# A gated MLP's adapters: two batches to a product in the ways out, both groups side by side in down's way in

## The chip, the cores and the metric

The kernel runs on one core of one Trainium2 chip. The metric is the device time of a run in microseconds (us); lower is better. Times given are the median of a few runs, and beside them stands one execution that the hardware profiler recorded.

## The reference, cut to what matters

The program is two transformer layers on 64 sequences (batches) of 32 tokens with 256 features, everything in float32. The part that is changed is the conditioning of the first layer's feed-forward: a gated MLP whose three projections each have a low-rank adapter of rank 16. Every batch has its own adapter, one of eight, chosen by an index that is known only at run time:

```python
def lora_linear(x, W, A, B, adapter_indices):
    base = einsum('bsd,df->bsf', x, W)
    lora = einsum('bsr,brf->bsf', einsum('bsd,bdr->bsr', x, A[adapter_indices]), B[adapter_indices])
    return base + lora

gate = lora_linear(x, Wg, Ag, Bg, i)      # 256 -> 1024
up   = lora_linear(x, Wu, Au, Bu, i)      # 256 -> 1024
y    = lora_linear(silu(gate) * up, Wd, Ad, Bd, i)   # 1024 -> 256
x    = x + ffn(y)
```

The text calls A the "way in" (features to 16 ranks) and B the "way out" (16 ranks to features). After this MLP come a quantised feed-forward (ffn), in the second layer a linear map with adapters, attention, a batch of experts and another quantised feed-forward.

## The kernel before, in words

The 2048 tokens are worked on in eight chunks of 256 tokens, that is of eight batches, and a chunk is two groups of four batches (128 tokens each). In a first half of some 790 us the kernel does the first layer's attention, in 32 steps. The second half is a pipeline written out by hand in `turn2(n)`: in turn n, chunk n goes through the gated MLP and the feed-forward, chunk n-1 through the second layer's attention, and chunk n-2 through its experts and last feed-forward, and the adapters of chunk n+1 are fetched. The order of the calls in `turn2` is the order of each engine's queue. A last function, `drain`, ends the chunks that are left. Chunk 0's gate and up products are done earlier, between the last steps of the first half (`chunk_0`).

Weights of the MLP (cgt, cut, cdt) stay in SBUF. The adapters don't: they are gathered anew for every chunk. `tabulate`, one piece at a time during the first half, writes two tables in DRAM with SP's DMAs: `alora`, whose row holds the ways in of gate, up and down for one feature and one adapter, and `blora`, whose rows hold the ways out of gate and up. `gather` (lines 431 and 433) copies a column of row numbers on VectorE (`at`) and then has GpSimd issue an indirect DMA. `fetch_in` gets the way in of one batch into the tile ag, `fetch_out` the ways out of one batch (128 rows of 1 KB) into the tile bx, and `fetch_down` down's way out for one group into bdt. In a turn these are eight, eight and two gathers. The row numbers (aidx, bidx, didx) are made once by `small_tables`, on VectorE, early in the first half.

The products concerned, all on TensorE:

- `adapters_in` (L472) brings the tokens to the ranks of gate and up; `adapters_spread` (L488) multiplies with a matrix fold of zeros and ones, which repeats the result in every block of 32 partitions, and masks it into u, so that gate's ranks stand in one half of the columns and up's in the other.
- `gate_up` (L507) does the full products of gate and up for one block of 128 features, and leaves the sum in a PSUM bank. Four blocks fill four banks.
- `gate_up_adapters` (L521) adds the ways out into those four banks: for each of eight batches and each of four blocks, one product with 32 rows (16 ranks of gate and of up), 128 columns of weights and 64 streamed columns (32 tokens for gate, 32 for up). The four blocks lie on four quarters of the partitions. Then ScalarE's Silu (L528) and VectorE's product (L529) make hT.
- `down_adapters` (L537) is down's way in: for two groups, eight blocks of features and four batches, one product with 16 columns of weights and 32 streamed ones, onto four quarters of the output partitions. VectorE copies the result (L546) to the diagonal blocks of ud, whose other blocks were set to zero once.
- `down` (L553) is the full product, and at its end (L559) the way out: four products with 128 columns of weights and 128 streamed ones.

Other lines that the text names: L1398 is `quant_up`, the gate and up product of the last feed-forward for chunk n-2, whose weights are y3T, a transposed tile that ScalarE copies out of PSUM (L395, `turn_y`). L1285 is the exponential of attention (`attn_exp`), L1233 a masked copy of the keys (kb), both on ScalarE. L1206 (`queries_keys`), L611 and L636 (the second layer's linear map) and L1242 (`project_values`, with its weights wv2, in the trace wv) are products that are not changed. L1047 is the last product of the first half's attention, and L1052 adds it to the tokens.

Of the kernel before, what the change touches and what calls it, by code (L numbers as in the profile page):

```python
# [15 lines left out]
P = 128  # L16
B = 64
# [8 lines left out]
for _name, _n in (  # L26
    ("ident", 128), ("pair", 64), ("cos", 32), ("sin", 32), ("cos4", 4),
    ("sin4", 4), ("causal", 32), ("blk4", 4), ("blk8", 8), ("quad", 4), ("p_mod32", 1), ("p", 1), ("p_mod16", 1),
    ("row16", 1), ("head2", 2), ("out_row", 1),
):  # L30
    _CONST[_name] = (_NCONST, _NCONST + _n)
    _NCONST += _n
# [6 lines left out]
def _constants():  # L39
# [30 lines left out]
    put("out_row", p // 32 * 256 + p // 16 % 2 * 128 + p % 16)  # L70
# [6 lines left out]
def mk_kernel(  # L77
# [61 lines left out]
    bidx = keep.tile([P, B], I32, tag="bidx", name="bidx")  # L139
    didx = keep.tile([P, NG], I32, tag="didx", name="didx")  # L140
    didf = keep.tile([P, NG], F32, tag="didf", name="didf")
# [5 lines left out]
    def small_tables():  # L147
# [7 lines left out]
        nc.vector.tensor_scalar(bidx, idx("lora"), 16.0, const("out_row"), MULT, ADD)  # L155

        folded = idx("expert")[:, :32]
        nc.vector.tensor_reduce(folded, ident.rearrange("p (r c) -> p c r", r=4), AX.X, ADD)
        nc.vector.tensor_copy(
            fold.rearrange("p (r c) -> p r c", r=4), folded.unsqueeze(1).to_broadcast([P, 4, 32])  # L160
        )
        own = idx("lora").rearrange("p (g b) -> p g b", b=4)
        of_group = keep.tile([P, NG, 4], F32, tag="m6", name="of_group")
        nc.vector.tensor_tensor(of_group, own, const("blk4").unsqueeze(1).to_broadcast([P, NG, 4]), MULT)
        nc.vector.tensor_reduce(didf, of_group, AX.X, ADD)
# [146 lines left out]
    blora = dram.tile([8 * P, 2 * P], F32, tag="blora", name="blora")  # L312
# [8 lines left out]
    def tabulate():  # L321
# [45 lines left out]
        for r in range(4):  # L367
            for i, src in enumerate((bg, bu)):
                rows = slice((2 * r + i) * P, (2 * r + i + 1) * P)
                nc.sync.dma_start(  # L370
                    out=blora[rows, :].rearrange("p (k f) -> p k f", k=2),
                    in_=src.rearrange("p (k r f) -> p k r f", k=2, r=4)[:, :, r, :],
                )
                yield
# [70 lines left out]
    def way_out(b):  # L445

        return mlp["bx", b // 4][:, b % 4 * 256 : (b % 4 + 1) * 256]

    def fetch_out(ch, b, held=True):
        gather(way_out(b), blora, bidx[:, ch * 8 + b : ch * 8 + b + 1], held)  # L450

    def fetch_down(ch, gi, held=True):

        g = ch * 2 + gi
        gather(bdt[:, gi, :], bd, didx[:, g : g + 1], held)
# [56 lines left out]
    def gate_up_adapters(ch, g):  # L512
# [4 lines left out]
        for b in range(8):  # L517
            cols = slice(b * T, (b + 1) * T)
            for r in range(4):
                rows = slice(32 * r, 32 * r + 32)  # L520
                nc.tensor.matmul(  # L521
                    banks[r].rearrange("p (i t) -> p i t", i=2)[:, :, cols],
                    lhsT=way_out(b)[rows, g * P : (g + 1) * P], rhs=c["u"][rows, :, cols],
                    start=False, stop=(b == 7),
                )
# [4 lines left out]

    def down_adapters(ch):
        c = chunks[ch]
        ps = bank()
        for gi in range(2):
            for k in range(8):
                for r in range(4):
                    nc.tensor.matmul(  # L537
                        ps[32 * r : 32 * r + 16, gi * T : (gi + 1) * T],
                        lhsT=way_in(gi * 4 + r)[:, 64 + k * 16 : 80 + k * 16],
                        rhs=c["hT"][:, k, gi * P + r * T : gi * P + (r + 1) * T],  # L540
                        start=(k == 0), stop=(k == 7),
                    )

        for r in range(4):
            rows = slice(32 * r, 32 * r + 16)
            nc.vector.tensor_copy(ud[rows, :, r, :], ps[rows, :64].rearrange("p (g t) -> p g t", g=2))  # L546

    def down(ch):
# [8 lines left out]
        for i in range(2):  # L557
            for gi in range(2):
                nc.tensor.matmul(  # L559
                    ps[:, i * 256 + gi * P : i * 256 + (gi + 1) * P], lhsT=bdt[:, gi, i * P : (i + 1) * P],  # L560
                    rhs=ud[:, gi, :, :].rearrange("p b t -> p (b t)"), start=False, stop=(i == 1 and gi == 1),
                )
# [85 lines left out]
    with ExitStack() as s1:  # L648
# [477 lines left out]
        for n in range(-1, len(steps) + 2):  # L1126
# [6 lines left out]
            if 28 <= n < 30:  # L1133
                fetch_out(0, 2 * (n - 28), False)
                fetch_out(0, 2 * (n - 28) + 1, False)
            if n == 30:
                for b in range(4, 8):
                    fetch_out(0, b, False)
# [17 lines left out]
    bdt = w.tile([P, 2, D], F32, tag="bdt", name="bdt")  # L1156
    for gi in range(2):
        fetch_down(0, gi, False)
    fetch_linear(0)
    ud = w.tile([P, 2, 4, T], F32, tag="ud", name="ud")  # L1160
    nc.gpsimd.memset(ud.rearrange("p g b t -> p (g b t)"), 0.0)
# [289 lines left out]
    def turn2(n):  # L1451
# [19 lines left out]
        for k in range(8):  # L1471
# [7 lines left out]
            elif k == 5:  # L1479
                on(n - 1, attn_exp)  # L1480
            elif k == 6:
# [55 lines left out]
        on(n + 1, fetch_out, 4)  # L1537
        on(n, ffn_down)
        on(n + 1, fetch_out, 5)
        on(n + 1, fetch_out, 6)  # L1540
        on(n + 1, fetch_out, 7)
# [7 lines left out]
        on(n + 1, fetch_down, 0)  # L1549
        on(n + 1, fetch_down, 1)  # L1550
# [126 lines left out]
```

## Time and profile before

| what | value |
|---|---|
| median of 3 runs | 1453.79 us (1450.05 to 1453.99) |
| the profiled execution's own time | 1451.43 us |
| its span, from the first to the last instruction | 1449.7 us |
| TensorE busy | 1399.7 us, 97% of the span |
| VectorE, ScalarE, GpSimd busy | 829.9, 614.1, 577.2 us |
| mean granted TensorE clock | 0.992 |
| gathers of ways in, ways out and down's way out, by the held row numbers | 954 ns of GpSimd each |

A row of the groups names the line, the engine, the operation, what is written and read, the shape (for a product rows times columns of weights and the streamed tile) and the number of instructions; behind the bar stand the busy time in us, the mean length of one in ns, and the idle time of the engine ahead of it with what ended it. PE is TensorE's multiplying, PEld its loading of weights, which overlaps it. Lengths of products overlap too, so that the time from one start to the next says more than a length.

### The profile page before, as it was taken

What the parts mean: (1) busy time and instruction counts of PE and PEld (TensorE: products, weight loads), DVE (VectorE), ACT (ScalarE), POOL (GpSimd) and SP (SyncE); (2) the same over time, 40 slices, a digit from 0 to 9 for tenths busy, and PEclk for the clock granted to TensorE, in tenths of its full rate; (3) what the DMA queues carried; (4) which work ended last, traced back from release to release, by engine and by line L of the source; (5) the groups of instructions that cost most, each with busy time, mean ns of one, the idle gap of its engine ahead of it and who ended that gap; (6) DMA issues with size and microseconds to landing.
All of it is one profiled execution on the core that took longest, in us unless ns stands there. A gap on an engine that the chain in (4) does not pass through costs nothing.

```text
span 1449.7 us, 39390 instructions
## 1 busy us (share of the span) xinstructions
PE 1399.7 (97%) x16552; PEld 1086.2 (75%) x16552; DVE 829.9 (57%) x1879; ACT 614.1 (42%) x2014; POOL 577.2 (40%) x650
## 2 busy tenths in 40 slices
PE   5899999999999999999999999999999999999996
PEld 3666777776767677767777788888887878788874
DVE  1566686867677776766565323363636262635554
ACT  1355665656575756565655512130312121212121
POOL 3423367777533333333445141524251606060320
PEclk9999999999999999999999999999999999999999
DMA  6201001321221000100001161313131304040220
GB/s 172 61 2 67 5 16 20 77 47 33 35 66 36 23 6 15 38 12 1 13 14 44 38 115 52 98 49 92 39 102 34 107 17 123 6 116 23 67 74 15
DMA packets 101625, 71.41 MB, mean 49 GB/s; under 512 B 71429, under 2 KB 88965, under 8 KB 101449
## 3 DMA queue, kind: packets, MB, share of 16 engines
q0 software_dynamic: 15744, 38.03, 9.5%
q1 hardware_dynamic: 82504, 26.34, 7.6%
q10 hardware_dynamic: 3200, 4.52, 1.0%
q8 instruction: 131, 2.15, 0.6%
q14 instruction: 46, 0.37, 0.1%
HBM read 64.54 MB, written 6.29 MB: 49 GB/s over the span
## 4 chain that ended last, share of the span: by engine, by line
PE 91%; DMA 3%; SPq 2%; DVE 2%; issue 1%; ACT 1%; POOL 0%; ACTq 0%; DVEq 0%
PE ps L779 16%; PE ps L810 15%; PE ps L1047 8%; PE ps L507 8%; PE ps L1398 5%; PE ps L578 4%; PE ps L553 3%; PE ps L1438 3%; PE ps L597 3%; PE ps L992 2%; PE ps L521 2%; PE ps L889 2%; PE ps L1206 2%; PE ps L1032 2%; SPq L276 1%; PE ps L967 1%
## 5 line engine op out<-in xcount | busy, mean ns | idle before, releaser
L433 POOL DMA_INDIRECT we<-in_ew,at x64 | 61.1, 955 | 277.5 <-DVE h L1405 203.7
L1001 ACT ACTIVATE sq<-ps 128x128 f32<-128x128 f32 x256 | 71.1, 278 | 211.6 <-PE ps L992 204.4
L793 POOL TENSOR_TENSOR qT<-ra,rb 128x256 f32<-128x256 f32 x64 | 46.6, 728 | 272.6 <-DVE rb L791 272.5
L1047 PE MATMUL ps<-wo,ogT 128*128 128x256 f32 x512 | 120.6, 389 | 6.1 <-DVE aT L896 6.1
L779 PE MATMUL ps<-hsT,wq 128*128 128x256 f32 x512 | 126.4, 390 | 0.0
L779 PE MATMUL ps<-hsT,wk 128*128 128x256 f32 x512 | 122.2, 382 | 0.0
L790 DVE TENSOR_TENSOR ra<-ps,ct 128x512 f32<-128x512 f32 x128 | 87.4, 683 | 49.9 <-PE ps L779 44.9
L810 PE MATMUL ps<-wv,hsT 128*128 128x512 f32 x256 | 115.2, 593 | 0.0
L810 PE MATMUL ps<-wg,hsT 128*128 128x512 f32 x256 | 115.1, 592 | 0.0
L1047 PEld LDWEIGHTS ps<-wo,ogT 128*128 128x128 f32 x512 | 95.8, 192 | 20.9 <-DVE aT L896 6.6
L779 PEld LDWEIGHTS ps<-hsT,wq 128*128 128x128 f32 x512 | 95.5, 192 | 18.3 <-issue 5.8
L873 DVE RECIPROCAL enz<-ps 128x256 f32<-128x256 f32 x64 | 107.5, 1721 | 2.7 <-PE ps L864 2.7
L779 PEld LDWEIGHTS ps<-hsT,wk 128*128 128x128 f32 x512 | 98.3, 192 | 13.7
L1010 POOL TENSOR_TENSOR f<-f,mhalf 128x8 f32<-128x8 f32 x32 | 53.1, 1660 | 133.5 <-DVE f L1008 133.5
L810 PEld LDWEIGHTS ps<-wg,hsT 128*128 128x128 f32 x256 | 48.6, 190 | 61.2 <-issue 54.3
L791 DVE TENSOR_TENSOR rb<-ps,ct 128x512 f32<-128x512 f32 x128 | 87.0, 680 | 0.0
L927 ACT ACTIVATE qv<-ok,nmx 128x64 f32<-128x64 f32 x256 | 85.0, 336 | 1.3 <-DVE nmx L923 1.3
L810 PEld LDWEIGHTS ps<-wv,hsT 128*128 128x128 f32 x256 | 48.6, 190 | 47.6 <-issue 45.9
L1398 PE MATMUL ps<-guT,y3T 128*128 128x352 f32 x256 | 79.5, 464 | 0.5 <-ACT y3T L395 0.5
L529 DVE TENSOR_TENSOR hT<-ps,sg 128x256 f32<-128x256 f32 x64 | 24.2, 419 | 96.9 <-ACT sg L528 96.9
L896 DVE SCALAR_TENSOR_TENSOR aT<-ps,ct 128x256 f32<-128x256 f32 x64 | 24.1, 419 | 85.6 <-PE ps L889 85.6
L433 POOL DMA_INDIRECT ag<-alora,at x56 | 53.4, 954 | 49.3 <-DVE at L431 39.3
(233 smaller groups left out, 3056.4 us busy)
## 6 DMA issues: line engine op xcount, KB each, us to landing
x<-in_x SPq DMA_DIRECT2D x8, 256.0 KB
wq<-in_wqT SPq DMA_DIRECT2D x16, 128.0 KB
wk<-in_wkT SPq DMA_DIRECT2D x16, 128.0 KB
wv<-in_wvT SPq DMA_DIRECT2D x4, 512.0 KB
wg<-in_wgT SPq DMA_DIRECT2D x4, 512.0 KB
wo<-in_woT SPq DMA_DIRECT2D x4, 512.0 KB
row<-in_wgu ACTq DMA_DIRECT2D x11, 128.0 KB
out<-res SPq DMA_DIRECT2D x5, 256.0 KB
```

Source lines behind the costliest of these rows:

```text
L433: nc.gpsimd.indirect_dma_start(out=to, out_offset=None, in_=table, in_offset=bass.IndirectOffsetOnAxis(ap=at, axis=0))
L507: nc.tensor.matmul(ps[:, i * 256 : (i + 1) * 256], lhsT=mlp[name, k // 4][:, j, part], rhs=c["xT"][:, j, :], start=(i == 0 and j == 0), st ...
L578: nc.tensor.matmul(ps[:, i * 256 : (i + 1) * 256], lhsT=wt[:, j, k * P : (k + 1) * P], rhs=yT[:, j, :], start=(j == 0), stop=(j == 1),)
L779: nc.tensor.matmul(ps[:, half * 256 : (half + 1) * 256], lhsT=wt[:, c, half * 256 + pr * P : half * 256 + (pr + 1) * P], rhs=hs[:, c, lo : ...
L790: nc.vector.tensor_tensor(by_t(a.rearrange("p h t -> p (h t)")), by_t(ps), cosb, MULT)
L791: nc.vector.tensor_tensor(by_t(b.rearrange("p h t -> p (h t)")), by_t(ps), sinb, MULT)
L810: nc.tensor.matmul(ps, lhsT=hs[:, c, lo + gi * P : lo + (gi + 1) * P], rhs=wt[:, c, :], start=(c == 0), stop=(c == 1),)
L873: nc.vector.reciprocal(t[:, e, :], banks[e][:, :256])
L927: nc.scalar.activation(qv[:, k, :], ok[:, k, :], AF.Exp, bias=nmx[:, k : k + 1], accum_out=rs[:, k : k + 1],)
L1001: nc.scalar.activation(sq, po[e][:, k * P : (k + 1) * P], AF.Square, accum_out=f[:, e * 4 + k : e * 4 + k + 1],)
L1047: nc.tensor.matmul(ps[:, gi * D : (gi + 1) * D], lhsT=s["ogT", gi][:, h, :], rhs=w[4][:, h, :], start=(h == 0), stop=(h == 3),)
L1398: nc.tensor.matmul(ps[:, :352], lhsT=c["y3T"][:, k, gi * P : (gi + 1) * P], rhs=guT[:, k, lo : lo + 352], start=(k == 0), stop=(k == 1),)
```

## The change

A product of the ways out now takes two batches. The table `blora` is laid out in halves, so that a gathered row holds four blocks of one half (2 KB); the gather brings two batches into 128 partitions, 64 for the blocks of even number and 64 for those of odd number, each 64 being two batches with gate's and up's 16 ranks. There are four gathers of 128 rows of 2 KB for a chunk instead of eight. fold repeats over 64 partitions instead of 32. The product has 64 rows, 128 columns of weights and 128 streamed columns (64 tokens each for gate and up), and two of the four banks' products lie on one half of the partitions.

For down's way in, a new function `pair_down` copies the ways in of both groups side by side on ScalarE (two copies of 128 x 512 into a new tile adp). It is called in the turn at k == 5, after `attn_exp`. A product then has 32 columns of weights (16 of each group) and 64 streamed columns (a batch of each group). Of the result only the blocks where group and batch fit are kept, by one VectorE product with a mask (own8) straight from PSUM into ud. Down's way out is gathered once for all eight batches (128 rows), and its product takes 256 streamed columns.

```diff
-    put("out_row", p // 32 * 256 + p // 16 % 2 * 128 + p % 16)
+    put("out_row", p // 64 * 256 + p // 16 % 2 * 128 + p % 16)
+    put("own8", (p[:, None] // 16 % 2 * 4 + p[:, None] // 32 == np.arange(8)[None, :]))
+    put("odd", (p[:, None] // 32 % 2 == np.arange(2)[None, :]))
...
-    blora = dram.tile([8 * P, 2 * P], F32, tag="blora", name="blora")
+    blora = dram.tile([4 * P, 4 * P], F32, tag="blora", name="blora")
...
-        for r in range(4):
+        for half in range(2):
             for i, src in enumerate((bg, bu)):
-                rows = slice((2 * r + i) * P, (2 * r + i + 1) * P)
+                rows = slice((2 * half + i) * P, (2 * half + i + 1) * P)
                 nc.sync.dma_start(
-                    out=blora[rows, :].rearrange("p (k f) -> p k f", k=2),
-                    in_=src.rearrange("p (k r f) -> p k r f", k=2, r=4)[:, :, r, :],
+                    out=blora[rows, :].rearrange("p (k f) -> p k f", k=4),
+                    in_=src.rearrange("p (k half f) -> p half k f", k=4, half=2)[:, half, :, :],
                 )
                 yield
...
-    def fetch_out(ch, b, held=True):
-        gather(way_out(b), blora, bidx[:, ch * 8 + b : ch * 8 + b + 1], held)
+    def fetch_out(ch, j, held=True):
+        gather(way_out(j), blora, bidx[:, ch * 4 + j : ch * 4 + j + 1], held)
...
-        for b in range(8):
-            cols = slice(b * T, (b + 1) * T)
+        for j in range(4):
+            cols = slice(j * 64, (j + 1) * 64)
             for r in range(4):
-                rows = slice(32 * r, 32 * r + 32)
+                rows = slice(r % 2 * 64, r % 2 * 64 + 64)
+                k = (4 * g + r) // 2
                 nc.tensor.matmul(
                     banks[r].rearrange("p (i t) -> p i t", i=2)[:, :, cols],
-                    lhsT=way_out(b)[rows, g * P : (g + 1) * P], rhs=c["u"][rows, :, cols],
-                    start=False, stop=(b == 7),
+                    lhsT=way_out(j)[rows, k * P : (k + 1) * P], rhs=c["u"][rows, :, cols],
+                    start=False, stop=(j == 3),
                 )
...
+    def pair_down(ch):
+
+        for gi in range(2):
+            nc.scalar.copy(
+                adp[:, :, :, gi, :],
+                mlp["ag", gi][:, :768].rearrange("p (r v) -> p r v", r=4)[:, :, 64:].rearrange(
+                    "p r (k i) -> p r k i", k=8
+                ),
+            )
+
     def down_adapters(ch):
+
         c = chunks[ch]
         ps = bank()
-        for gi in range(2):
-            for k in range(8):
-                for r in range(4):
-                    nc.tensor.matmul(
-                        ps[32 * r : 32 * r + 16, gi * T : (gi + 1) * T],
-                        lhsT=way_in(gi * 4 + r)[:, 64 + k * 16 : 80 + k * 16],
-                        rhs=c["hT"][:, k, gi * P + r * T : gi * P + (r + 1) * T],
-                        start=(k == 0), stop=(k == 7),
-                    )
-
-        for r in range(4):
-            rows = slice(32 * r, 32 * r + 16)
-            nc.vector.tensor_copy(ud[rows, :, r, :], ps[rows, :64].rearrange("p (g t) -> p g t", g=2))
+        for k in range(8):
+            for r in range(4):
+                nc.tensor.matmul(
+                    ps[32 * r : 32 * r + 32, :64].rearrange("p (g t) -> p g t", g=2),
+                    lhsT=adp[:, r, k, :, :].rearrange("p g i -> p (g i)"),
+                    rhs=c["hT"][:, k, :].rearrange("p (g r t) -> p r g t", g=2, r=4)[:, r, :, :],
+                    start=(k == 0), stop=(k == 7),
+                )
+        nc.vector.tensor_tensor(
+            ud, ps[:, :64].rearrange("p (g t) -> p g t", g=2).unsqueeze(2).to_broadcast([P, 2, 4, T]),
+            const("own8").rearrange("p (g r) -> p g r", g=2).unsqueeze(3).to_broadcast([P, 2, 4, T]), MULT,
+        )
...
         for i in range(2):
-            for gi in range(2):
-                nc.tensor.matmul(
-                    ps[:, i * 256 + gi * P : i * 256 + (gi + 1) * P], lhsT=bdt[:, gi, i * P : (i + 1) * P],
-                    rhs=ud[:, gi, :, :].rearrange("p b t -> p (b t)"), start=False, stop=(i == 1 and gi == 1),
-                )
+            nc.tensor.matmul(
+                ps[:, i * 256 : (i + 1) * 256], lhsT=bdt[:, i * P : (i + 1) * P],
+                rhs=ud.rearrange("p g b t -> p (g b t)"), start=False, stop=(i == 1),
+            )
...
             elif k == 5:
                 on(n - 1, attn_exp)
+                on(n, pair_down)
...
-        on(n + 1, fetch_down, 0)
-        on(n + 1, fetch_down, 1)
+        on(n + 1, fetch_down)
```

The calls of `fetch_out` for the batches 4 to 7 fall away in the turn, and so do those of chunk 0 in the first half. ud's setting to zero falls away. `small_tables` makes the row numbers for pairs and for whole chunks, with two more small VectorE instructions.

## The prediction

> **What bounds the kernel now.** I read the page's busy times first, then busy time by stretch, then the waits and the chain of one turn of the second half, and last the groups of the products that the change touches.
>
> ```profile
> PE 1399.7 (97%) x16552; PEld 1086.2 (75%) x16552; DVE 829.9 (57%) x1879; ACT 614.1 (42%) x2014; POOL 577.2 (40%) x650
> ```
>
> TensorE is busy for 97% of the span. A share of the whole says little, so the stretch of one turn (they repeat every 76.3 us) and one of the last stage; columns after the window are its length and the busy us of PE, PEld, DVE, ACT, POOL:
>
> ```profile
> 1006.00:1082.00 76.00, 75.91 (x1015) 63.65 (x1014) 36.32 (x103) 16.53 (x36) 27.05 (x29) 1.00 0.24 68
> ...
> 1386.00:1449.70 63.70, 48.87 (x464) 35.74 (x462) 33.37 (x73) 14.44 (x28) 1.91 (x2) 0.92 0.07 22
> ```
>
> In a turn PE is idle for 0.09 us of 76; VectorE, ScalarE and GpSimd have half of it or more free. All that PE waits for between 860 and 1370 us is one line of the waits:
>
> ```profile
> PE ps L537 <- DVE hT L529: 2.2, 2, 1.9
> ```
>
> So only what shortens or delays PE's own queue counts; fewer gathers and fewer VectorE copies are not worth anything by themselves. The chain of that turn (start, us, what) prices the products concerned:
>
> ```profile
> 1014.66 1.94 PE ps L521 x64
> ...
> 1027.41 1.94 PE ps L521 x64
> 1029.36 4.93 PE ps L1398 x16
> 1034.29 1.32 PE ps L537 x88
> ...
> 1047.45 0.89 PE ps L559 x8
> ...
> 1074.52 0.36 PE ps L611 x16
> ...
> 1076.87 0.69 PE ps L636 x8
> ```
>
> Every product in the source is two MATMUL instructions here (L521: 32 products, x64). L611 and L636 are not changed; they have the forms that the new products will have. The weight loads behind them:
>
> ```profile
> L521 PEld LDWEIGHTS ps<-u,bx 32*128 32x128 f32 x1024 | 30.0, 186 | 5.0 <-issue 5.0
> L1206 PEld LDWEIGHTS ps<-wqk,eT 128*32 128x32 f32 x1024 | 27.8, 110 | 1.4 <-ACT eT L642 1.4
> L636 PEld LDWEIGHTS ps<-xa,ag 64*128 64x128 f32 x64 | 4.2, 186 | 1.0
> ```
>
> A load of 128 columns takes 186 ns whether it has 32 rows or 64; one of 32 columns takes 110.
>
> **What the Trainium skill says.** "TensorE: Matmul & The Clock Gate", section "LDWEIGHTS (loading the stationary operand)", says that a load's time goes by its columns, not its rows. The two 186s agree. "TensorEngine Tiling (Array Packing)", section "Tiling Modes", gives four independent tiles for 32 rows by 128 columns and two for 64 by 128, loading and multiplying in parallel. The trace agrees: at L521 the starts come in groups of four some 7 ns apart, at L636 in groups of two, and from one group to the next it is 112 ns in both.
>
> **The change, part by part.**
>
> *Ways out (L521, 16 calls).* Each call goes from 32 products of 32 rows x 64 streamed columns to 16 of 64 rows x 128 columns. Half the instructions looks like half of 1.94 us. But four ran at once and now two do: 64/4 = 16 groups before, 32/2 = 16 groups after. What is a group's pace? Before, the stream is not the limit: L611 streams 64 columns and its groups start 56 ns apart, while L521 needs 112, so it is the 128-column load that sets it. After, the load is as long, and the stream of 128 columns has grown to about 110 (L1206, 128 columns with a small load: its groups start 110.6 ns apart). L636 has just this form (64 rows, 128 columns of weights, 128 streamed) and its groups start at 112 ns. Hence 16 x 112 before and after. Only the first group is dearer: 213 ns to the second group at L636 against 160 at L521, so +0.05 a call, 16 calls: **+0.85 us**.
>
> *Down's way in (L537, 8 calls).* From 64 products of 16 columns x 32 streamed to 32 of 32 columns x 64 streamed: 128 instructions in 1.32 us become 64. L611 has the new form: 4 groups in 0.36 us, 56 ns from one to the next. 16 groups: 0.36 + 12 x 0.056 = 1.03. Gain 0.29 a call. In turn 1 more: there PE stands 1.9 us for hT's last blocks and then still has the second group of batches to do (hT ends at 892.57, L553 starts at 893.63, so 1.06 after). With both groups in one pass only the last block's eight instructions remain, some 0.25: gain 0.8. In turn 0 nothing: what follows is set by a load. In the chain of turns 0 and 1 the transfer of wv (issued at 862.42, landing at 868.2, its queue started by L1047's end) holds L1242 up, and PE would only wait longer there. So 6 x 0.29 + 0.8 = **-2.55 us**.
>
> *Down's way out (L559).* Eight instructions of 128 streamed columns in 0.89 us become four of 256; L507 and L553 run 256 at 0.216 each: 4 x 0.216 = 0.86. Seven turns that count: **-0.2 us**.
>
> *The added pair_down.* Two ScalarE copies of 128x512 from SBUF to SBUF, after attn_exp and before turn_y's copy y3T, which L1398's first weight load waits for. Behind them in ScalarE's queue: y3T, then Silu's table load and four Silus. The place in the timeline:
>
> ```profile
> 1026.53 1.06 ACT L1285 ACTIVATE sc<-sc 128x1024 f32<-128x1024 f32 x1 [6.83 <-DVE sc L1279]
> 1027.50 0.57 ACT L395 COPY y3T<-ps 128x512 f32<-128x512 f32 x1
> 1029.29 4.44 PEld L1398 LDWEIGHTS ps<-guT,y3T 128*128 128x128 f32 x16
> 1029.42 1.28 ACT L528 ACT_TABLE_LOAD   x1 [1.35 <-PE ps L521]
> ```
>
> y3T ends at 1028.06 and is wanted at 1029.29; some 0.05 passes from an end to PE's start (in the last stage, y3T's end 1432.84 to L1398's 1432.89). So 1.17 us are free. A copy of duration c takes c - 0.09 of the queue (y3T starts 0.09 before Exp ends). It stalls PE once 2(c - 0.09) > 1.17, that is c > 0.68. The trace has no SBUF-to-SBUF copy of this shape. From below: the PSUM copies of 128x512 take 0.57 to 0.64. From above: kb (L1233), SBUF to SBUF in blocks and scaled by a tile, takes 0.72, giving 0.09 a turn. The 16-element runs of adp could cost more, and Exp's 1.06 for twice the elements is the worst that a row suggests: 0.77 a turn. I take 0.65 to 0.72, so 0 to 0.09 in each of turns 2 to 7: **+0.2 us** (ends 0 and +4.6). The Silus aren't delayed: the table load waits for L521's end at 1029.4, and y3T is through by 1029.3. In turn 0 the copies run from 831.8 (the last Silu) to about 833.1, and L537 starts at 833.69, so nothing. In turn 1 no y3T follows and Exp ends at 885.83, three microseconds before the Silus. That the copies wait for ag's gathers costs nothing: these were issued a turn earlier, and L472 has read them 25 us before.
>
> *Gathers, VectorE, first half.* Four gathers of 2 KB rows replace eight of 1 KB, one for down replaces two: five fewer a turn at 0.95 us of GpSimd and 0.14 of VectorE. Hidden before (PE waits for no gather), so no gain; four ud copies of 0.22 become one product of about 0.42, equally hidden. The first half's small tables gain two VectorE instructions of about 0.22 each between 96 and 98.5 us; VectorE then idles 2.44 until 100.94, which covers them. The table of ways out is written by four larger DMAs instead of eight, same bytes and same 512-byte runs, all ahead of their first gather; the ones queued behind them on SP (cgt, cut) move earlier, not later. ud's memset goes.
>
> *Sum:* 0.85 - 2.55 - 0.2 + 0.2 = **-1.7 us**. The profiled execution's own time is 1451.43 (span 1449.7); with -1.7 it would be 1449.7. The median of the three runs, 1453.79, lies 2.4 above it; the forecast is set against that: 1452. I call up to 0.3% (4.4 us) no change; the three runs differ by 3.9.
>
> **Rivals.**
>
> *Half the instructions, half the time.* If two loads at once took half of what four take, groups of two would start 56 ns apart: 0.21 to the second group, 14 x 0.056 and 0.2 from the last one's start to the next product make 1.2 a call instead of 1.94, 16 x 0.74 = -11.9 us. With -2.55 - 0.2 + 0.2 that is -14.5: 1439. For it: weight loads are the limit now. Against: L636 runs exactly this form at 112 ns, and L1206 shows that 128 streamed columns alone need 110.
>
> *Copies that hold y3T up (slower).* If short runs make pair_down's copies twice kb's 0.72, that is 1.45, each of turns 2 to 7 stalls for 2 x 1.36 - 1.17 = 1.55, and turn 0 for 0.8 (copies until 834.5): +10.1, and with the other parts' -1.9 it ends near 1462. It cancels the gain from c = 0.83, and is measurably slower from 1.2. For it: nothing in the trace writes 64-byte runs from ScalarE. Against: L422's scattered copy takes 0.64, only 0.05 over plain ones.
>
> *Pairs that don't overlap*: 32 x 0.112 a call instead of 16 adds 1.8, 29 us in all: 1481. L636's starts 6 ns apart speak against it.
>
> **How the numbers follow.** The sum near -1.7: 0.76, of which run-to-run scatter (3.9 us over three runs) and the clock after turn 1's gap (four matmuls at 427 ns instead of 216, L553, which may come or go) put 0.60 within 0.3%, 0.11 below, 0.05 above. Half the time: 0.10, faster. Late y3T: 0.10, of it 0.04 within. No overlap: 0.04. Together faster 0.21, same 0.64, slower 0.15. The range takes Exp's price for the copies (-1.9 + 4.6: 1456.5) and the scatter: 1446 to 1458, leaving out the first and last rivals and the far end of the second.
>
> **What would show it.** Right: the chain has the ways out at 1.9 to 2.0 us with x32 instead of x64, down's way in near 1.03 with x64, y3T's end just ahead of L1398's first load, PE's idle time in a turn still near 0.1. Wrong: ways out near 1.3 (first rival); PE waiting at the gate product for y3T in six turns, copies over 0.83 (second); starts at the ways out never less than 50 ns apart (third).

## The result, and the profile after

The changed kernel takes 1446.40 us (median of 21 runs, 1443.92 to 1450.11) against 1450.18 for the kernel before, timed beside it (21 runs, 1448.01 to 1453.99). The ratio is 0.9972, with an interval of 0.9964 to 0.998: 3.8 us or 0.28% less, just within what the prediction calls no change. The profiled execution has a span of 1444.3 us and an own time of 1446.06.

TensorE's line on the page, by which both kernels stand at 97%, has 1056 MATMUL instructions fewer and only 4.6 us less of busy time:

```profile
PE 1395.1 (97%) x15496; PEld 1080.3 (75%) x15496; DVE 823.6 (57%) x1822; ACT 622.4 (43%) x2030; POOL 538.5 (37%) x609
```

The stretch of a turn (window, its length, then busy us of PE, PEld, DVE, ACT, POOL, and last the clock, DMA share and GB/s) has PE as full as before. GpSimd's busy time has fallen from 27 to 22 us, and ScalarE's has grown by one, the added copies:

```profile
1002.00:1078.00 76.00, 75.90 (x898) 63.38 (x890) 35.76 (x94) 17.56 (x38) 22.26 (x24) 1.00 0.24 65
```

PE's waits from 860 to 1370 us are still one line. No wait for y3T stands beside it, so pair_down's copies hold nothing up:

```profile
PE ps L559 <- DVE hT L541: 1.7, 2, 1.5
```

The chain through one turn (start, us, what):

```profile
1024.47 1.99 PE ps L533 x32
1026.45 4.93 PE ps L1417 x16
1031.38 1.03 PE ps L559 x64
...
1044.25 0.86 PE ps L580 x4
...
1047.34 1.28 PE ps L1329 x65
1048.62 0.04 issue
1048.66 0.55 PE ps L1329 x21
```

L533 is the ways out (L521 before), L559 down's way in (L537), L580 its way out (L559 before), L1329 `attn_values` (L1310). Half the instructions of the ways out take 0.05 us more, the way in takes 1.03 instead of 1.32. The weight loads of the new products, by form, show why the first is so; the load of 128 columns has not become cheaper with 64 rows:

```profile
L533 PEld LDWEIGHTS ps<-u,bx 64*128 64x128 f32 x512 | 29.8, 188 | 5.0 <-issue 5.0
...
L559 PEld LDWEIGHTS ps<-hT,adp 128*32 128x32 f32 x512 | 7.7, 110 | 5.8 <-DVE rs L1311 3.0 <-DVE hT L541 2.4 <-issue 0.3
```

I cut TensorE's records of both profiles into stages, each from its first start to the next stage's, and added them up from the first ways out on. This stretch takes 636.79 us before and 632.94 after. The other 1.5 us of the 5.4 by which the two spans differ lie ahead of it, where TensorE runs the same 8406 MATMULs in both kernels.

| stage | before, us | after, us | difference | predicted |
|---|---|---|---|---|
| ways out, 16 calls | 31.09 | 31.76 | +0.67 | +0.85 |
| down's way in, 8 calls | 13.73 | 10.84 | -2.89 | -2.55 |
| down's way out, 8 calls | 7.13 | 6.91 | -0.22 | -0.2 |
| stall of the gate product for y3T | 0 | 0 | 0 | +0.2 |
| `attn_values`, 8 calls, not edited | 16.46 | 14.78 | -1.68 | 0 |
| down's full product, not edited | 56.95 | 57.25 | +0.30 | 0 |
| sum | | | -3.8 | -1.7 |

So the parts that were edited give -2.4, and a product that nobody touched gives 1.7 more. The chain of the kernel before shows that stage, 2.18 us long from PE's first start to the next stage's:

```profile
1050.56 1.02 PE ps L1310 x50
1051.59 0.03 issue
1051.62 1.13 PE ps L1310 x41
1052.74 1.28 PE ps L578 x5
```

"issue" is PE waiting for nothing that the profile shows. The piece is only 0.03 us long; the pauses themselves show when the starts of PE's records are read one by one. GpSimd's timeline of the kernel before, round that stage:

```profile
1049.54 0.95 POOL L433 DMA_INDIRECT ag<-alora,at  x1 [0.30 <-PE ps L390]
1050.48 0.33 POOL L568 MEMSET gT<- 64x256 f32 x1
1050.98 0.96 POOL L433 DMA_INDIRECT ag<-alora,at  x1 [0.17 <-issue]
1052.25 0.95 POOL L433 DMA_INDIRECT we<-in_ew,at  x1 [0.30 <-issue]
```

and of the changed kernel, whose stage starts at 1047.28:

```profile
1046.26 0.33 POOL L589 MEMSET gT<- 64x256 f32 x1
1046.76 0.96 POOL L444 DMA_INDIRECT ag<-alora,at  x1 [0.17 <-ACT xT L406]
1048.02 0.95 POOL L444 DMA_INDIRECT we<-in_ew,at  x1 [0.30 <-issue]
```

Before, two gathers start inside the stage (0.49 and 1.76 us after its first product); after, one (0.74 after), and the one ahead of it starts 0.51 us before the stage. PE's records have a gap between two starts in the stage near each gather's start and again some 0.4 us later, where the stage lasts that long: before, 0.17 us at 1051.00, 0.24 at 1051.38, 0.21 at 1052.19; after, 0.13 at 1048.02 and 0.25 at 1048.40. VectorE executes nothing during the stage in either trace. My theory from there on: the gathers pause PE's run of short products, and the change gains by having moved them 1.0 us earlier against PE. About half of this 1.0 is VectorE's, which makes the gathers' row numbers behind the ud step: four copies in 0.91 us before, one product in 0.41 after. The rest I did not trace. The rival is that the stage is shorter because fewer instructions stand ahead of it in PE's queue.

One of the eight calls is another matter. The last, in `drain`, has no gather near it and still takes 1.84 us before and 1.76 after. There the trace's clock record has half speed for 3.41 us, from 1401.64 before and from 1396.58 after. Where the clock is full, that call takes 1.39 to 1.40 (e1, e9).

### The profile page after: what moved, and what is told of

The parts are those of the page before. It is cut to its first block, busy times and chain, and to the rows that moved or that the text cites. A ratio compares the mean times of both kernels' runs of the same rounds, so it can differ in the third digit from the quotient of the medians.

```text
span 1444.3 us, 37162 instructions
## 1 busy us (share of the span) xinstructions
PE 1395.1 (97%) x15496; PEld 1080.3 (75%) x15496; DVE 823.6 (57%) x1822; ACT 622.4 (43%) x2030; POOL 538.5 (37%) x609
## 3 DMA queue, kind: packets, MB, share of 16 engines
HBM read 63.49 MB, written 6.29 MB: 48 GB/s over the span
## 4 chain that ended last, share of the span: by engine, by line
PE 91%; SPq 2%; DMA 2%; DVE 2%; issue 1%; ACT 1%; POOL 0%; ACTq 0%; DVEq 0%
PE ps L800 16%; PE ps L831 15%; PE ps L1068 8%; PE ps L518 8%; PE ps L1417 5%; PE ps L599 4%; PE ps L575 3%; PE ps L1457 3%; PE ps L618 3%; PE ps L1013 2%; PE ps L533 2%; PE ps L910 2%; SPq L287 2%; PE ps L1225 2%; PE ps L1053 2%; PE ps L988 1%
## 5 line engine op out<-in xcount | busy, mean ns | idle before, releaser
L800 PEld LDWEIGHTS ps<-hsT,wq 128*128 128x128 f32 x512 | 95.5, 192 | 18.3 <-issue 6.0
L1417 PE MATMUL ps<-guT,y3T 128*128 128x352 f32 x256 | 79.5, 464 | 0.5 <-ACT y3T L406 0.5
L541 DVE TENSOR_TENSOR hT<-ps,sg 128x256 f32<-128x256 f32 x64 | 24.3, 420 | 95.7 <-ACT sg L540 95.7
L599 PE MATMUL ps<-yT,f 128*128 128x256 f32 x320 | 71.2, 382 | 0.2 <-ACT yT L585 0.2
```

The lines of the kernel that those rows point to most:

```text
L599: nc.tensor.matmul(ps[:, i * 256 : (i + 1) * 256], lhsT=wt[:, j, k * P : (k + 1) * P], rhs=yT[:, j, :], start=(j == 0), stop=(j == 1),)
L800: nc.tensor.matmul(ps[:, half * 256 : (half + 1) * 256], lhsT=wt[:, c, half * 256 + pr * P : half * 256 + (pr + 1) * P], rhs=hs[:, c, lo : ...
L1417: nc.tensor.matmul(ps[:, :352], lhsT=c["y3T"][:, k, gi * P : (gi + 1) * P], rhs=guT[:, k, lo : lo + 352], start=(k == 0), stop=(k == 1),)
```

## The experiments

The first four and the last three ran where the kernel before takes 1450 us. The four between (e5 to e8) ran on a chip where it takes 1652.27 (1645.29 to 1653.19, 9 runs). There only ratios and stages are read, and their stages are compared with those of the faster chip, since neither the kernel before nor the changed kernel has a profile on the slower one.

### e1: the ways out alone

From the changed kernel, with down's part (the copies, ways in and out, ud's step and its gathers) as before:

```diff
-                on(n, pair_down)
...
-        on(n + 1, fetch_down)
+        on(n + 1, fetch_down, 0)
+        on(n + 1, fetch_down, 1)
```

> The ways out alone, with their table, fold and four gathers of 2 KB rows; down's adapters as before. Theory A (a group of products costs one 128-column weight load, 112 ns, whether four or two run at once): each of the 16 calls takes 1.985 us against 1.943, so +0.7 us; the total within 0.1% of before, if anything slower. Rival B (half the instructions are worth time by themselves): calls well under 1.94 and a total lower by 5 us or more. Theory C (a gather that GpSimd issues pauses TensorE's short products at L1310): L1310 changes from 2.18 us a turn only if the gathers that fall into it move; four gathers fewer come after L1310 in the turn, so it should stay at 2.0 to 2.2.

1449.33 us (14 runs), ratio 0.9993 (0.9984 to 1.0002): level with before. The ways out take 1.98 to 1.99 a call, the same +0.67 in sum; the way in stays at 1.32. `attn_values` is 2.0 us in four of the turns 2 to 6 and 1.56 in one, instead of 2.16 to 2.19. With four gathers less the others start 0.20 us earlier against PE in the four, and in the one a gather starts just as the stage does. That is 1.3 us less in these five turns. In this one trace the stage of L1242 in turn 0, which waits for a load, takes 3.20 us instead of 2.12, and the span from the first ways out on is 636.77, as before.

### e2: down's part alone

From the kernel before, with the changed kernel's `pair_down`, `down_adapters`, `down` and single gather of bdt; the ways out and their eight gathers stay:

```diff
+                on(n, pair_down)
...
-        on(n + 1, fetch_down, 0)
-        on(n + 1, fetch_down, 1)
+        on(n + 1, fetch_down)
```

> Down's adapters alone (pair_down, both groups in one pass, one gather, way out in one block); ways out as before. Theory A: way in 1.03 us instead of 1.32 in seven turns and about 1 us less in turn 1, way out 0.03 less a turn: -3.1 us. Theory C adds that L1310 falls from 2.18 to about 1.87 us in turns 2 to 6 because VectorE's shorter ud step and the missing wait on down's products start the gathers earlier, so that one fewer falls into L1310: -1.6, in all -4.5 to -4.7, better than the whole change (-3.8). Rival: L1310's gain belongs to the ways out's fewer gathers; then L1310 stays at 2.18 here and the total is -3.

1446.99 us (22 runs), ratio 0.9982 (0.9973 to 0.9991), 2.6 us by the ratio and 3.0 by the medians. The way in takes 1.03 and, in turn 1, 3.96; the ways out keep 1.94; and `attn_values` falls to 1.90 to 1.92 in turns 2 to 6, again 1.3 us less in sum. The gathers start 0.78 us earlier against PE; with e1's 0.20 that makes the 1.0 of the whole change. The stage came as the theory had it, but the total did not: the forecast was 4.5 to 4.7 us, and 3 was the rival's. In the trace, turn 1's full product takes 9.52 us here instead of 8.40, with the clock at half speed for 6.83 us instead of 3.41; whether that explains the difference in the medians is not shown. So both parts move the gathers, down's part further, and each shortens the untouched stage. The ways out alone, with their own +0.67, come out level on this chip.

### e3: what sets the pace of the ways out

In the first call of a turn, all products but those of the last two batches stream 64 columns; in the second they load 64 columns of weights and stream 128. Both leave out half of those products' work:

```diff
+                if j < 3 and g == 0:
+                    nc.tensor.matmul(to[:, 0, cols], lhsT=way_out(j)[rows, k * P : (k + 1) * P],
+                                     rhs=c["u"][rows, 0, cols], ...)
+                elif j < 3:
+                    nc.tensor.matmul(to[:64, :, cols], lhsT=way_out(j)[rows, k * P : k * P + 64],
+                                     rhs=c["u"][rows, :, cols], ...)
```

> Changed kernel whose ways out leave work out: in the first of the two calls of a turn the first three pairs of batches stream only gate's 64 columns, in the second they load only 64 of the 128 columns of weights; the last pair is complete in both. If the load of 128 columns sets the pace, halving the stream changes nothing (groups start 112 ns apart, call 1.9 to 2.0 us). If the stream sets it, they start 56 ns apart. Halving the weights: if the stream of 128 columns is a second limit of the same height, groups still start 107 to 112 ns apart; if not, some 60. I expect about 110 in both calls.

A single run, 1444.75 us. The chain has the two calls as

```profile
1011.29 1.49 PE ps L535 x24
1012.78 0.50 PE ps L545 x8
...
1024.09 1.46 PE ps L540 x24
1025.55 0.65 PE ps L545 x8
```

and the weight loads, by form, as

```profile
L535 PEld LDWEIGHTS ps<-u,bx 64*128 64x128 f32 x192 | 11.3, 187 | 2.5 <-issue 2.5
L540 PEld LDWEIGHTS ps<-u,bx 64*64 64x64 f32 x192 | 10.3, 133 | 2.5 <-issue 2.5
```

With half the stream (L535) the groups still start 111 to 112 ns apart; with half the load, 133 ns instead of 187 (L540), 109 to 110 apart. Neither half alone gains anything: the load of 128 columns and the stream of 128 columns are two limits at nearly one height, so that 32-row products with 64 streamed columns, 64-row ones with 128, and both of these halves all take the same time. The 133 and 187 for 64 and 128 columns agree in direction with the Trainium skill, "TensorE: Matmul & The Clock Gate", section "LDWEIGHTS (loading the stationary operand)", which has a load's time go by its columns. They do not follow its formula, by which half the columns take half the time: here they take 0.71 of it.

### e4: the copies of pair_down twice

```diff
-        for gi in range(2):
+        for gi in (0, 1, 0, 1):
```

> Changed kernel with pair_down's two copies made twice (four copies of 0.60 us in ScalarE's queue instead of two). In the changed kernel y3T ends 0.44 us ahead of the gate product's first matmul, of which some 0.05 is the signal's way: 0.39 free. Two more copies take 2 x 0.51 = 1.03 of the queue. If y3T is what the gate product waits for next, PE stalls 0.64 us in each of turns 2 to 7: +3.8 us against the changed kernel, about level with before. If something else covers it (no wait on y3T): same time as the changed kernel.

The stall came, in six turns, as PE's waits show:

```profile
PE ps L1417 <- ACT y3T L406: 3.5, 6, 0.6
...
PE ps L559 <- DVE hT L541: 0.4, 2, 0.3
```

The ways out with that wait last 2.63 to 2.64 instead of 1.99 in turns 2 to 7: +3.9. Yet the time did not go back to that of the kernel before, as I had expected with such a stall. It is level with the changed kernel's: 1446.29 (22 runs), ratio 0.9979 (0.997 to 0.9987). The second line says where it was given back: PE's wait for hT in turn 1 is gone. ScalarE's timeline there, first the changed kernel's,

```profile
883.79 1.12 ACT L546 COPY adp<-ag 128x512 f32<-128x512 f32 x2
887.26 1.28 ACT L540 ACT_TABLE_LOAD   x1 [2.34 <-PE ps L533]
888.55 0.66 ACT L540 ACTIVATE sg<-ps 128x256 f32<-128x256 f32 x2
```

then this one's:

```profile
882.60 2.16 ACT L546 COPY adp<-ag 128x512 f32<-128x512 f32 x4
884.77 1.28 ACT L540 ACT_TABLE_LOAD   x1
886.07 0.66 ACT L540 ACTIVATE sg<-ps 128x256 f32<-128x256 f32 x2
```

In the changed kernel the load of Silu's table waits until the ways out are done (2.34 us idle for L533), and then delays hT by its 1.28. In e4 it starts directly behind the copies, and only Silu itself waits. As the traces have it, the table load carries the wait on PE in the changed kernel and none in e4. The way in of turn 1 falls from 3.62 to 2.33, and the full product behind it from 8.70 to 7.01. In the changed kernel the clock record has half speed from 891.41 to 894.82, two us after PE's wait of 1.5, and in it seven MATMULs of that product start 427 ns after the one before instead of 216. In e4 the wait is 0.3 us, and the clock stays full. Those two stages are -3.0. A stage of the last turns' quantised feed-forward (L1457) takes 2.69 instead of 3.69, because the half speed from 1396.58 on, which the changed kernel's trace has there, is missing in e4's; that makes the rest.

### e5 and e6: the two gathers of k == 4 behind attn_values

In the changed kernel (e5) and in the kernel before (e6):

```diff
-        on(n + 1, fetch_in, 4)
-        on(n - 1, fetch, 4)
...
         for k in range(4):
             on(n - 1, attn_values, k)
+        on(n + 1, fetch_in, 4)
+        on(n - 1, fetch, 4)
```

> Changed kernel with two gathers of a turn (the fifth way in and the fifth expert) asked for behind the attention's value products instead of ahead of them, so that none is issued while those short products (L1329) run. Theory C (an issuing gather pauses short products twice, some 0.13 and 0.25 us in the changed kernel's trace): L1329's stage falls from 1.87 to about 1.5 us in turns 1 to 7, -2.3 to -2.6 us in all against the changed kernel. Rival (the pauses belong to the product stream itself, such as the fetching of instructions): the pauses stay where they are and the time with them.

> The kernel before with the same move of two gathers. Theory C: L1310's stage falls from 2.18 to about 1.5 us in turns 2 to 6 (three pauses of 0.17, 0.24 and 0.21 go) and by 0.35 in turns 1 and 7, about -3.7 us, as much as the whole change brought. Rival (pauses of the stream itself): 2.18 stays.

e5: 1584.88, ratio 0.9587 (0.957 to 0.9603). `attn_values` takes 1.40 to 1.41 in turns 2 to 6, where no gather starts in it, with no gap over 0.09; in turn 7 one gather starts 0.83 us ahead of it and it takes 1.68, with a gap of 0.20; in turn 1 three start in it and it takes 6.57. e6: 1633.43 (4 runs), ratio 0.9891 (0.9876 to 0.9906). Here the last gather starts 0.95 us ahead of the stage and ends as the stage begins. The stage takes 1.85 to 1.90 in turns 2 to 6, with one gap of 0.49 to 0.61 some 0.2 us in, and not the 1.5 expected; in turn 1 it takes 6.29. The products and their order are the same, and the length goes by where the gathers are. The absolute times expected were for the other chip and can't be judged here.

What sets this chip apart is in the page's line and in PE's waits of all the span, of e6:

```profile
PE 1482.3 (91%) x16552; PEld 1141.3 (70%) x16552; DVE 829.5 (51%) x1879; ACT 616.4 (38%) x2014; POOL 576.3 (35%) x650
...
PE ps L889 <- issue: 45.5, 74, 1.6
PE ps L967 <- issue: 13.4, 18, 1.2
PE ps L1438 <- issue: 12.7, 19, 1.4
```

The span of 1630.7 us is 181 us longer than that of the kernel before on the faster chip. PE is idle for 98 us more in it, and busy for 83 more with the same 16552 MATMULs. The clock record has half speed for 204 us of it and for 26 of the other, so the longer busy time goes with the slower clock.

L889 and L967 are products of the first half's attention, in steps where GpSimd gathers the tables' rows one after another; L1438 stands at the end of a turn, where it gathers bx, eb and bdt. These three add up to 71.6 us, and PE's nine longest waits in the kernel before, on the chip of 1450 us, have none of them. The steps of the first half show where most of the time goes. Eight steps with nine gathers each take 34.4 to 36.4 us in e6 and 23.3 to 24.3 in the kernel before; the ten steps behind them, with none, take 23.6 in both, and from 475 to 720 us e6's PE has no wait at all.

At the end of a turn, L1438's MATMULs in e6 start 0.7 to 1.4 us apart for a while (1213.03 to 1217.23), amid twelve gathers (1207.52 to 1227.74); the 24 of L597 ahead of them still keep 0.22, though the first of these gathers are under way. I take it that TensorE's instructions come late, but the traces don't show it. The transfers that they mark as instructions take as long in e6 as in the kernel before (131 packets on one queue, 1.06 and 1.08 us on average).

### e7 and e8: Silu's table load brought forward

A copy of one column, written again, behind pair_down's two; it waits only for ScalarE's own work, as e4's extra copies do. e7 is the changed kernel with it, e8 is e2's kernel with it and with e5's later gathers:

```diff
+        nc.scalar.copy(adp[:, 0, 0, 1, :1], mlp["ag", 1][:, 64:65])
```

> Changed kernel with a third ScalarE copy of one column, of a value that is there already, at the end of pair_down. It makes ScalarE wait for its own earlier work at that place, so that the Silu behind it has one wait left, which then stands on the Silu and no longer on the table load. Theory: the load of 1.28 us starts right after the copies instead of at the ways out's end; in turn 1, where PE waits 1.5 us for hT, PE's wait falls to 0.3 and the slowed clock that follows it (down's full product 8.7 us instead of 6.9) goes: -1.2 to -2.7 us against the changed kernel. In turns 2 to 7 nothing, since PE has the experts' product to do meanwhile; y3T moves 0.2 later within its 0.39. Rival (the even time of the kernel with the copies made twice is scatter): no gain.

> What the runs so far point to: down's adapters as in the change, ways out as before (0.04 us a call cheaper), the two gathers moved, and the one-column copy. Parts against before: down's adapters -3.1, gathers -3.7, table load -1.2 to -2.7: 1440 to 1442 us where before has 1450. Rival: the parts overlap (they shift each other's gathers), and it ends with the best single one, near 1444.

e7: 1586.70, ratio 0.9611 (0.9596 to 0.9625), level with e5; turn 1's way in takes 2.29 instead of 3.63 (e5), the full product behind it 7.01 instead of 8.70. Its gathers are where the changed kernel has them, and on this chip the stage pays more for them. PE's waits have a line that e5's lack:

```profile
PE ps L1330 <- issue: 17.1, 22, 1.1
```

With one gather starting 0.66 us into it and one 0.6 ahead of it, as in the changed kernel, `attn_values` (L1330) takes 3.80 to 4.24 in turns 2 to 6, against e5's 1.40. Yet the two kernels are level. In all eight calls e5 is 18.3 us shorter here, and 14.7 longer in the down product of the last feed-forward (L1457, 59.96 us in e5 and 45.31 in e7). So on this chip most of what the later gathers take out of one stage comes back at another.

e8: 1618.36, ratio 0.9792 (0.9778 to 0.9805), with `attn_values` at 1.40 to 1.41 in turns 2 to 6 and turn 1's way in at 2.50. It has both edits, lacks the changed ways out of e5 and e7 with their fewer gathers, and takes 32 to 33 us longer: what is worth nothing by itself on one chip is worth 2% on the other. Steps 28 to 31 of the first half, where TensorE's program is the same in all four (8406 MATMULs stand ahead of the first way out in each kernel), take 26.7, 28.3, 28.4 and 25.0 us in e6 and e8 (eight gathers of bx) and 24.7, 24.6, 23.7 and 23.8 in e5 and e7 (four). So 11.6 of the 32 to 33 us arise where only the gathers and their table differ.

### e9: both edits together, e11: the changed kernel again, e10: fewer gathers alone

e9 has e5's and e7's edits. e10 is the kernel before with four gathers of ways out less in a turn and TensorE's program unchanged:

```diff
-        on(n + 1, fetch_out, 4)
         on(n, ffn_down)
-        on(n + 1, fetch_out, 5)
-        on(n + 1, fetch_out, 6)
-        on(n + 1, fetch_out, 7)
```

> Both single edits in the changed kernel together: the two gathers of k == 4 behind attn_values, and the early copy that brings Silu's table load forward. Theory (the gathers' issues cause the pauses in attn_values; the table load causes the rest of the wait in turn 1): attn_values L1330 at 1.40 to 1.45 instead of 1.86 in turns 1 to 5 (-2.2 us) and turn 1's way in at 2.3 to 2.5 instead of 3.62 (-1.2 us), what follows in turn 1 up to 1.5 shorter when the clock holds. On a chip where the kernel before takes 1450: about 3.4 us below the changed kernel, 1442 to 1443.5, ratio to before 0.994 to 0.9955. On the chip where it takes 1652: at or below the 1585 of the kernels with one of the two edits. Rival (the two stages are shortened only for a wait to come back at the next stage): stages as said, the time level with the changed kernel's, within 1 us.

> The changed kernel itself, on the chip of the two others. On a chip where before takes 1450: 1446 to 1447 with attn_values L1329 at 1.86 and turn 1's way in at 3.62. On the chip where it takes 1652: if the gathers' place within attn_values costs there too, some 3 us above the 1585 of the kernel with the later gathers; if only their number counts, level with it.

> The kernel before without four of the eight gathers of ways out in a turn (batches 4 to 7 keep the first chunk's ways out, so those batches' products use the wrong weights). TensorE's program is unchanged, instruction for instruction. Theory (what the change saves on a chip with slow delivery is gathers, not TensorE instructions; where delivery keeps up, fewer gathers at the end of the turn are worth nothing): on a chip where before takes 1450, within 1 us of it, with attn_values L1310 still at 2.16 to 2.19, since the two gathers in it are left; on the chip where it takes 1652, 20 to 35 us less. Rival (TensorE's own fewer instructions make the difference there): within 5 us of before on either chip.

This time before took 1449.99 (19 runs). e9: 1440.06 (5 runs), ratio 0.9936 (0.9923 to 0.9949), with no wait brought back:

```profile
1044.14 1.40 PE ps L1330 x82
```

in the chain, and of the wait for hT 0.3 us left in PE's waits. GpSimd issues nothing from before this stage until well behind it:

```profile
1042.94 0.33 POOL L590 MEMSET gT<- 64x256 f32 x1
1047.86 0.96 POOL L444 DMA_INDIRECT ag<-alora,at  x1 [4.59 <-issue]
```

TensorE has the changed kernel's products in the changed kernel's order (15496 MATMULs), so the rival, fewer instructions ahead of the stage, is out. In turn 1 a gather still starts in the stage, and it takes 1.89 there, not the 1.40 to 1.45 expected. e11: 1444.80 (5 runs), ratio 0.9967 (0.9955 to 0.998), `attn_values` at 1.87 and turn 1's way in at 3.63. This is 1.6 us less than the same kernel's 1446.40 in the first comparison and below the 1446 to 1447 expected, so two medians of one kernel can lie that far apart here. Against e11 the two edits together are worth 4.7 us more, and e9 beats both kernels; what each is worth alone on this chip was not timed. I had expected 3.4; the stages of `attn_values` (14.88 to 11.71 in all eight calls, the last turn's and the drain's too), of turn 1's way in (3.63 to 2.29) and of the product behind it (8.70 to 7.01) make 6.2 in the profiles, of which the medians show three quarters. Of the 6.2, 0.36 is the drain's call, which met the half clock in e11 and not in e9.

e10: 1449.14 (14 runs), ratio 0.9996 (0.9986 to 1.0005), level, as theory and rival alike have it on this chip; `attn_values` stayed at 2.16 to 2.17 in four turns, since the gathers in it stayed, and fell to 1.91 in one, where one gather starts in it, at 0.88 us, instead of two. That fewer gathers at the end of a turn are worth nothing here is shown. How the rest of e8's 32 to 33 us divides between gathers and TensorE's fewer instructions in the turns stays open: e10 was timed on the faster chip alone.

## Why the prediction was right, point by point

The forecast of no measurable change held, and so did its mechanism for the products that were edited, but 1452 was 5.6 us too high. That it held is in part luck: 3.8 us is close to the 4.4 that it calls no change, 1446.40 lies 0.4 above the low end of its range, and 1.7 us came from a stage that it put at nothing. Two thirds of the 5.6 is the base: it was set against three runs with a median of 1453.79, and with 18 more the median is 1450.18. The other 2.1 is the sum, -1.7 against -3.8.

- *Ways out, +0.85.* Right in kind: 16 groups of 112 ns before and after (e3 shows both limits). The first group cost 0.04 more instead of 0.05: +0.67.
- *Way in, -2.55.* The 0.29 of turns 2 to 6 is exact; turn 7 had only 0.16 to give. Turn 1 gave 0.98 instead of 0.8. In turn 0 the step "PE would only wait longer there" failed: its 0.29 was kept, and the stage L1242 is 2.12 in both profiles. That load's landing varies by more than this: the stage is 3.20 in e1 and 1.73 in e2 and e9.
- *Way out, -0.2.* -0.22 measured.
- *pair_down, +0.2.* The copies took 0.601 and 0.612, less than the 0.65 to 0.72 I took; y3T's copy started at 1025.37 and was through 0.44 before L1417's first product, so no stall, and 0 instead of 0.2. ScalarE's timeline:

```profile
1024.34 1.12 ACT L546 COPY adp<-ag 128x512 f32<-128x512 f32 x2
1025.37 0.58 ACT L406 COPY y3T<-ps 128x512 f32<-128x512 f32 x1
1026.30 1.28 ACT L540 ACT_TABLE_LOAD   x1 [0.36 <-PE ps L533]
```

- *Gathers and VectorE, "no gain".* This is the step that failed. It read that PE waits for no gather's data, which is so. It did not ask what a gather does to PE while GpSimd issues it, or that the change would move the gathers against PE. The chain of before has an "issue" piece within L1310, but of 0.03 us; the pauses of 0.17 to 0.24 were to be seen in the starts alone. Worth -1.68, nearly all that the sum lacked.
- *Turn 1's clock.* Named as scatter, and it went the wrong way by 0.3. The starts 427 ns apart are five before and seven after, not four.

The rivals: half the time for half the instructions is refuted by L533's 1.99 and by e3. Late y3T did not come with two copies and came with four; its price, 0.65 a turn, is what the slack says, but e4's end shows that a stall in one place can be paid for by a wait that goes elsewhere, which the rival left out. Pairs overlap: starts of a pair are 5 to 7 ns apart.

## What to carry to other kernels

Before halving the number of products on TensorE, count groups that run at once and ask for two limits, the weight load by its columns and the stream by its own: if both stand near each other, fewer products of a wider tile with a longer stream took as long here (e1, e3). Whether fewer instructions help by themselves on the slower chip stays open. Read the starts inside runs of short products, not only the chain's "issue" pieces, and lay GpSimd's timeline beside them: with two gathers moved behind such a run, its seven calls in the turns took 2.8 us less in the trace (e9 against e11). On the slower chip most of such a gain came back as a wait elsewhere, so look at the total too. And where an activation's table load waits, look whether it must: work of ScalarE's own ahead of it can let it start while TensorE is still busy.

## What the runs showed of the hardware that I had not expected

- A gather on GpSimd goes with pauses of 0.11 to 0.25 us in a run of TensorE's short products, near its start and again some 0.4 us later, with no semaphore between them. On the faster chip `attn_values` at full clock takes 1.40 us with no gather starting in it, 1.84 to 1.92 with one that starts 0.4 us or more into it, and with two 2.00 to 2.19 in most turns. It goes by the gather's place as well as by the number: a gather at 0.2 us and one at 1.5 leave 1.78 to 1.86 (turn 1), and one that starts just as the stage does, with a second at 1.44, leaves 1.56 (one turn of e1). What in the gather does it was not found.
- One chip differs from the other by 14% on the same kernel (1652 against 1450). In the first half e6 loses time in the steps where gathers are issued one after another (34.4 to 36.4 us for 23.3 to 24.3) and none in the ten steps without gathers (23.6 on both), and its clock is at half speed for 204 us instead of 26. In e7 `attn_values` takes 3.80 to 4.24 there with the gathers placed as in the changed kernel. The changed kernel itself was not timed there; with later gathers it is 4.1% faster than before, with the early table load 3.9%. Why the chips differ was not found.
- A short wait of TensorE was enough for a spell at half clock. In turn 1, all seven traces of the faster chip in which PE's starts lie 1.7 to 2.1 us apart at the wait for hT have half speed for 3.41 or 6.83 us within some two us of its end; the two in which they lie 0.5 apart (e4, e9) have none there.
- Copies of 128x512 within SBUF in runs of 16 elements cost ScalarE 0.60 to 0.62 us, as much as its copies from PSUM (0.57 to 0.64).
